# A ternary feed-forward sublayer whose last product runs in two float32r halves instead of one float32 product

## The chip, the cores and the metric

The kernel runs on one core of a Trainium2 chip. The metric is the device time of one execution, in microseconds (us). A core has five engines that matter here, each with its own in-order queue: PE (the matrix engine; its weight loads have a row of their own, PEld), DVE (VectorE), ACT (ScalarE), POOL (GpSimd) and SP, which only issues DMAs here. Engines wait for each other by semaphores. PE's results land in PSUM, from where DVE and ACT take them.

## The reference

The program is a decoder of four layers with three sublayers each (attention, cross attention, feed-forward) on x of 64 x 64 rows and width 256, that is 4096 rows. After each sublayer comes `x = layernorm(x + sublayer(x))`. The change is in the sixth sublayer, the feed-forward of the second layer:

```python
def _L1_ffn_ref(x, W_g, W_u, W_d):
    def rms_norm(x, eps=1e-8):
        mean = jnp.mean(x, axis=-1, keepdims=True)
        var = jnp.var(x, axis=-1, keepdims=True)
        return (x - mean) / jnp.sqrt(var + eps)
    def activation_quant(x):
        s = 127.0 / jnp.max(jnp.abs(x), axis=-1, keepdims=True)
        return jnp.clip(jnp.round(s * x), -128, 127) / s
    def ternary_matmul(x, w):
        return jnp.matmul(x, jnp.sign(w).T)
    xq = activation_quant(rms_norm(x))
    p = jax.nn.silu(ternary_matmul(xq, W_g)) * ternary_matmul(xq, W_u)
    return ternary_matmul(p, W_d)
```

All three weights are used by their signs only (-1, 0 or 1). The hidden width is 1024. The rows xq are whole numbers times one scale per row, so the first two products are exact in bf16; the gated rows p are full float32 numbers.

## The kernel before

The 4096 rows are eight groups of 512 (`NTOK`), four tiles of 128 each (`TG`). The hidden width is eight chunks of 128 (`HC`). `l1_ffn` walks over 64 units (group g, chunk i), one a step, and each step records work for several units at different stages:

- `hidden(g, i)` (L1378 to L1381): four bf16 products of 512 columns on PE give the PSUM banks "gate" and "up", DVE multiplies gate by the row scales into the SBUF tile `hid` (L1380), ACT applies Silu in place (L1381).
- `gated` one step later (L1386): DVE multiplies `hid` by "up", in place.
- `down` two steps behind `hidden` (L1396): for each of the four row tiles, PE takes 128 columns of `hid` as stationary weights and streams 256 columns of the signs of W_d, both float32, and adds into the PSUM tiles `acc` over the eight chunks. One float32 product of the program stands as two LDWEIGHTS and two MATMUL in the trace.
- `ends` of a finished group, spread over the steps of the next: `sums` (L1411, DVE: z = acc * scale + x), statistics (L1417, L1419), `root` (L311 on DVE and a power on POOL, L313), `apply` (L1428 on ACT).
- `first.quantize` of a later group, in three parts at the steps i = 6, 2 and 5: row statistics on DVE (L339, L342, L311) and then on POOL a power (L313) and four normalisations (L228); row maxima on DVE (L233 to L236) and four roundings on POOL (L240); clipping on DVE (L243, L244). `first.turn` (L266 to L275) then transposes a group's quantized rows.

The order on PE and DVE in this stage is the order in which the code records it (`manual_schedule`); ACT, POOL and SP are ordered by a planner, but each runs its own queue in order. The end of the cross attention's last group (`inverted`, `fetched`, `added`, `normalized`, L1280 to L1300: a reciprocal on DVE, two DMAs, then two products of 1024 columns and four normalisations on POOL) falls into the first steps of this stage.

The signs are made during the cross attention (`L1Ffn.weights`, L207 and L210): twelve pieces of 512 columns, POOL compares with 0 from below, one step later DVE compares from above and subtracts. The signs of W_g and W_u go to a bf16 tile, those of W_d are written over the float32 weight. All weight tiles come from `ring`, a pool of eight slots of 2048 float32 columns; the loads of the following sublayer's weights (`l2_wqkv`, `l2_wsg`) wait for slots of it. `l2_wqkv` is also scaled once on DVE (L1507) while the cross attention still runs.

The pool tiles `hid` have five buffers, the PSUM banks gate and up four together, `acc` two.

Of the kernel before, what the change touches and what calls it, by code (L numbers as in the profile page):

```python
# [9 lines left out]

F32 = mybir.dt.float32
BF16 = mybir.dt.bfloat16
FP8 = mybir.dt.float8e4
I32 = mybir.dt.int32
AF = mybir.ActivationFunctionType
ALU = mybir.AluOpType
# [3 lines left out]
P = 128  # L20
# [3 lines left out]
NTOK = TG * P  # L24
# [3 lines left out]
WCOLS = 2048  # L28
# [3 lines left out]
class Linear:  # L32
# [68 lines left out]
    def first(self, pool, bank, fill):  # L101
# [74 lines left out]
class L1Ffn:  # L176
# [9 lines left out]
    def load(self):  # L186

        dec, names = self.dec, ("l1_wg", "l1_wu", "l1_wd")
        self.raw = [dec.weight(name) for name in names]
        both = dec.ring.tile([P, 2, WCOLS], BF16, tag="w", name="l1_signs")  # L190
        self.out = [both[:, 0], both[:, 1], self.raw[2]]
        self.signs = []
        for w, out, name in zip(self.raw, self.out, names):
            n = dec.ins[name].shape[1]
            dec.load(w.rearrange("p (c n) -> p c n", n=n), dec.ins[name].rearrange("(c p) n -> p c n", p=P))
            self.signs.append(out.rearrange("p (c n) -> p c n", n=n))

    def weights(self):

        nc, N = self.nc, 512  # L200
        chunks = [(w[:, c : c + N], out[:, c : c + N]) for w, out in zip(self.raw, self.out) for c in range(0, WCOLS, N)]
# [77 lines left out]
class Decoder:  # L279
# [1082 lines left out]
    def l1_ffn(self, ctx, shared, later, first):  # L1362
# [7 lines left out]
        wg, wu, wd = first.signs  # L1370
        state = first.state

        def hidden(g, i):
            xt, rows, _ = state[g]
            pg, pu = self.bank("gate"), self.bank("up")
            for ps, w in ((pg, wg), (pu, wu)):
                for c in range(2):
                    nc.tensor.matmul(ps, w[:, c, i * P : (i + 1) * P], xt[:, c, :], start=c == 0, stop=c == 1)  # L1378
            h = wk.tile([P, NTOK], F32, tag="hid", name="hid", bufs=5)
            nc.vector.tensor_tensor(h, pg, rows, ALU.mult)  # L1380
            nc.scalar.activation(h, h, AF.Silu)  # L1381
            state[g, i] = h, pu

        def gated(g, i):
            h, pu = state[g, i]
            nc.vector.tensor_tensor(h, h, pu, ALU.mult)  # L1386

        def down(g, i):

            h = state.pop((g, i))[0]  # L1390
            if i == 0:
                state[g, "acc"] = [
                    self.psum.tile([P, 2, D], F32, tag="acc", name="acc", bufs=2) for _ in range(2)
                ]
            for t in range(TG):
                nc.tensor.matmul(  # L1396
                    state[g, "acc"][t // 2][:, t % 2, :], h[:, t * P : (t + 1) * P], wd[:, i, :],
                    start=i == 0 and t % 2 == 0, stop=i == HC - 1, skip_group_check=True,
                )

        def ends(g):

            x, am, acc = self.X[g], state.pop(g)[2], state.pop((g, "acc"))
            z = wk.tile([P, TG, D], F32, tag="z", name="z")
            mv = self.smallp.tile([P, TG, 2], F32, tag="bnmv", name="bnmv", bufs=4)
            st = self.smallp.tile([P, TG, 6], F32, tag="bnst", name="bnst", bufs=4)
            rstd, nb = self.small(TG, "rstd", bufs=4), self.small(TG, "nmr", bufs=4)

            def sums():
                for t in range(TG):  # L1410
                    nc.vector.scalar_tensor_tensor(  # L1411
                        z[:, t, :], acc[t // 2][:, t % 2, :], am[:, t : t + 1], x[:, t, :], ALU.mult, ALU.add
                    )

            def statistics(ts):
                for t in ts:
                    nc.vector.bn_stats(st[:, t, :], z[:, t, :])  # L1417
                for t in ts:
                    nc.vector.bn_aggr(mv[:, t, :], st[:, t, :])  # L1419

            def root():
                statistics((2, 3))
                self.rsqrt(rstd, mv[:, :, 1], 1.0, 1e-5)

            def apply():
# [1117 lines left out]
```

## Time and profile before

| | |
|---|---|
| device time, median of 3 runs | 4253.46 us (4248.44 to 4256.29) |
| span of the profiled execution, first to last instruction | 4250.0 us |
| mean granted PE clock of that execution | 0.986 |
| feed-forward stage: first and last L1380 on DVE | 1135.0 and 1314.3 us |
| PE busy in the span | 4051.5 us, 95% |
| DVE, ACT, POOL busy in the span | 3042.7, 2106.4, 1506.3 us |

Times of instructions count from the span's start. A busy share is an average over stages with different limits, so the stage is read by itself in windows of one group's length. "Idle before" is the time in which an engine waited before an instruction, with what ended that wait. MATMUL records overlap: a record lasts longer than the distance to the next start, and it is the distance that the engine needs for one.

### The profile page before, as it was taken

How to read it: one execution, taken by the hardware profiler on the slowest of the kernel's cores; microseconds unless marked ns; L12 is line 12 of the kernel's file. 1: busy time of each engine (PE TensorE's matmuls, PEld its weight loads, DVE VectorE, ACT ScalarE, POOL GpSimd, SP SyncE). 2: the span in 40 equal slices, each digit the busy share in tenths (PEclk: the TensorE clock that was granted, in tenths of full speed). 3: DMA queues.
4: the chain of work that ended last, by engine and by line, in shares of the span. 5: the costliest groups of instructions: out<-in, count | busy, mean ns of one | idle time of the engine just before them, and what ended most of it. 6: DMA issues, size and time to landing. Idle time of an engine off the chain costs nothing.

```text
span 4250.0 us, 74130 instructions
## 1 busy us (share of the span) xinstructions
PE 4051.5 (95%) x28788; PEld 2618.4 (62%) x28808; DVE 3042.7 (72%) x6107; ACT 2106.4 (50%) x3863; POOL 1506.3 (35%) x1553
## 2 busy tenths in 40 slices
PE   8889999989998999989999999999999999999998
PEld 5645556666675555546666666666656666666666
DVE  6844548888685688877777777777766777777786
ACT  5555635767634577544444444444433444444443
POOL 4511112242341111115555555555544444444111
PEclk9989999999999999999999999999999999999999
DMA  2200002333300000031111111111131100000000
GB/s 81 73 21 10 1 26 69 72 84 71 82 1 12 1 1 1 10 132 28 26 31 26 26 31 26 26 30 27 26 102 28 26 23 21 23 23 16 11 16 18
DMA packets 108294, 144.00 MB, mean 34 GB/s; under 512 B 15844, under 2 KB 73380, under 8 KB 106536
## 3 DMA queue, kind: packets, MB, share of 16 engines
q1 hardware_dynamic: 106984, 137.69, 12.7%
q8 instruction: 228, 3.74, 0.4%
q10 hardware_dynamic: 960, 1.57, 0.2%
q14 instruction: 122, 1.00, 0.1%
HBM read 70.25 MB, written 26.76 MB: 23 GB/s over the span
## 4 chain that ended last, share of the span: by engine, by line
PE 65%; DVE 15%; ACT 6%; POOL 4%; issue 3%; DMA 1%; SPq 0%; POOLq 0%; ACTq 0%; DVEq 0%
PE p L1777 19%; PE acc L2066 5%; PE acc L2274 4%; PE sq L1208 3%; PE ret L1247 2%; PE qT L319 2%; PE acc L1396 2%; POOL rstd L313 2%; DVE bnst L339 2%; PE gate L911 2%; DVE mc L1213 2%; PE gate L1592 2%; PE sk L1211 2%; PE s L2004 2%; PE up L911 2%
## 5 line engine op out<-in xcount | busy, mean ns | idle before, releaser
L313 POOL TENSOR_TENSOR rstd<-rstd,neg_half 128x1 f32<-128x1 f32 (+1 forms) x195 | 157.9, 810 | 653.1 <-DVE rstd L311 585.2
L313 POOL TENSOR_TENSOR hrq<-hrq,neg_half 128x4 f32<-128x4 f32 x256 | 258.7, 1011 | 300.7 <-DVE hrq L311 283.9
L1213 DVE TENSOR_REDUCE mc<-sq 128x2 f32<-128x512 f32 x512 | 317.1, 682 | 63.9 <-PE sk L1211 63.7
L1219 ACT ACTIVATE e<-sk 128x512 f32<-128x512 f32 x512 | 265.5, 608 | 112.1 <-PE sk L1211 111.5
L1208 PE MATMUL sq<-l1x 32*128 32x256 f32 x2048 | 275.2, 407 | 4.9 <-DVE z L1094 3.1
L1777 PE MATMUL p<-l3a_wq,xt 128*128 128x512 f32 x512 | 243.8, 599 | 11.2 <-DVE v L300 9.9
L313 POOL TENSOR_TENSOR hrk<-hrk,neg_half 128x4 f32<-128x4 f32 x160 | 188.2, 1176 | 185.8 <-DVE hrk L311 181.0
L1211 PE MATMUL sk<-l1x 32*128 32x256 f32 x2048 | 252.9, 392 | 0.0
L1777 PE MATMUL p<-l3a_wk,xt 128*128 128x512 f32 x512 | 247.1, 605 | 0.0
L1208 PEld LDWEIGHTS sq<-l1x 32*128 32x128 f32 x2048 | 208.3, 195 | 58.8 <-issue 23.6
L1777 PE MATMUL p<-l3x_wq,xt 128*128 128x512 f32 x512 | 242.3, 596 | 0.3 <-DVE k L2168 0.3
L1777 PE MATMUL p<-l3a_wv,xt 128*128 128x512 f32 x512 | 233.9, 599 | 0.4 <-ACT y L94 0.4
L2274 PE MATMUL acc<-l3x_wo,yt 128*128 128x256 f32 x1024 | 232.4, 380 | 1.6 <-DVE yt L300 1.0
L2066 PE MATMUL acc<-l3a_wproj,yt 128*128 128x256 f32 x1024 | 232.0, 379 | 0.5 <-DVE yt L300 0.5
L2066 PEld LDWEIGHTS acc<-l3a_wproj,yt 128*128 128x128 f32 x1024 | 194.2, 190 | 53.7 <-issue 29.2
L2274 PEld LDWEIGHTS acc<-l3x_wo,yt 128*128 128x128 f32 x1024 | 190.5, 190 | 33.9 <-issue 7.7
L1211 PEld LDWEIGHTS sk<-l1x 32*128 32x128 f32 x2048 | 188.5, 187 | 7.3 <-issue 2.9
L2237 POOL TENSOR_TENSOR s<-s,smx 128x512 f32<-128x512 f32 x64 | 66.9, 1046 | 333.8 <-DVE smx L2236 319.8
L319 PEld LDWEIGHTS qT<-ident,q 128*128 128x128 f32 x1024 | 121.9, 141 | 95.9 <-issue 75.2
L2050 POOL TENSOR_TENSOR hry<-hry,neg_half 128x8 f32<-128x8 f32 x64 | 106.2, 1659 | 183.4 <-DVE hry L2046 183.4
L319 PE MATMUL qT<-ident,q 128*128 128x128 f32 x1024 | 157.4, 277 | 3.3 <-ACT qT L2208 2.4
L1247 PE MATMUL ret<-e,vt 128*32 128x256 f32 x2048 | 140.6, 390 | 18.2 <-DVE mc L1213 17.2
(415 smaller groups left out, 10209.4 us busy)
## 6 DMA issues: line engine op xcount, KB each, us to landing
vs<-v SPq DMA_DIRECT2D x308, 128.0 KB
l3x_kv<-kv SPq DMA_DIRECT2D x28, 256.0 KB
x<-in_x SPq DMA_DIRECT2D x8, 512.0 KB
ct<-in_ctxT SPq DMA_DIRECT2D x8, 512.0 KB
cn<-in_ctx SPq DMA_DIRECT2D x8, 512.0 KB
l1x<-in_ctx SPq DMA_DIRECT2D x128, 32.0 KB
l1x_x<-x SPq DMA_DIRECT2D x8, 512.0 KB
l1x<-l1x_x SPq DMA_DIRECT2D x128, 32.0 KB
```

Source lines behind the costliest of these rows:

```text
L313: nc.gpsimd.tensor_tensor(out, out, self.neg_half[:, :n], ALU.pow)
L319: self.nc.tensor.transpose(ps[:, j * P : (j + 1) * P], blk, self.ident)
L911: nc.tensor.matmul(ps[:n], w[:, c, h0 : h0 + n], xt[:, c, :], start=c == 0, stop=c == 1)
L1208: nc.tensor.matmul(ps[:, n, :], x_[rows, j, part], c_[rows, j, :], start=True, stop=True)
L1211: nc.tensor.matmul(ps[:, n, :], c_[rows, j, part], x_[rows, j, :], start=True, stop=True)
L1213: nc.vector.tensor_reduce(mc[new % 2][:, ra + k, 2 * j : 2 * j + 2], ps, AX.X, ALU.max, negate=True)
L1219: nc.scalar.activation(es[rb + k], ps, AF.Exp, scale=scale)
L1247: nc.tensor.matmul(ret[32 * r : 32 * r + 32, :], vt[i % 2][:, lc, 4 * r + j, :], es[r][:, lc, :], start=lc == 0, stop=lc == 1,)
L1777: self.nc.tensor.matmul(ps, lhs(c), w(c, cols), start=c == 0, stop=c == 1 and bias is None)
L2050: nc.gpsimd.tensor_tensor(r, r, self.neg_half[:, :8], ALU.pow)
L2066: nc.tensor.matmul(acc[:, :D], yts[h % 2][:, h // 2, :], wp[n // 8][:, (n % 8) * D : (n % 8 + 1) * D], start=n == 0, stop=n == 15,)
L2274: nc.tensor.matmul(acc[:, :D], yts[h % 2][:, h // 2, :], w.o[n // 8][:, (n % 8) * D : (n % 8 + 1) * D], start=n == 0, stop=n == 15,)
```

## The change

The signs of W_d go to a new tile of type float32r from the ring, asked for when the ninth piece is made. [...] `down` makes two float32r products, one for each half, where there was one float32 product, and stands three steps behind `hidden` instead of two. `sums` moves from step 1 to step 2 of the next group. `hid` has four buffers, `hhi` two, `hlo` three.

```diff
 class L1Ffn:  # load
-        self.out = [both[:, 0], both[:, 1], self.raw[2]]
+        self.out = [both[:, 0], both[:, 1], None]
...
         def step(i):
             if i < len(chunks):
+                k, cols = chunks[i]
                 below[i] = self.shared.tile([P, N], F32, tag="below", name="below", bufs=2)
-                nc.gpsimd.tensor_scalar(below[i], chunks[i][0], 0.0, None, ALU.is_lt)
+                nc.gpsimd.tensor_scalar(below[i], self.raw[k][:, cols], 0.0, None, ALU.is_lt)
             if i > 0:
-                w, out = chunks[i - 1]
-                nc.vector.scalar_tensor_tensor(out, w, 0.0, below[i - 1], ALU.is_gt, ALU.subtract)
+                k, cols = chunks[i - 1]
+                if self.out[k] is None:
+                    self.out[k] = self.dec.weight("l1_wd_signs", F32R)
+                nc.vector.scalar_tensor_tensor(
+                    self.out[k][:, cols], self.raw[k][:, cols], 0.0, below[i - 1], ALU.is_gt, ALU.subtract
+                )
...
-            h = wk.tile([P, NTOK], F32, tag="hid", name="hid", bufs=5)
+            h = wk.tile([P, NTOK], F32, tag="hid", name="hid", bufs=4)
...
         def gated(g, i):
-            h, pu = state[g, i]
+            h, pu = state.pop((g, i))
             nc.vector.tensor_tensor(h, h, pu, ALU.mult)
+            hi, lo = (wk.tile([P, NTOK], F32R, tag=n, name=n, bufs=b) for n, b in (("hhi", 2), ("hlo", 3)))
+            nc.scalar.copy(hi, h)
+            nc.gpsimd.tensor_tensor(lo, h, hi.bitcast(F32), ALU.subtract)
+            state[g, i] = hi, lo
...
             for t in range(TG):
-                nc.tensor.matmul(
-                    state[g, "acc"][t // 2][:, t % 2, :], h[:, t * P : (t + 1) * P], wd[:, i, :],
-                    start=i == 0 and t % 2 == 0, stop=i == HC - 1, skip_group_check=True,
-                )
+                for k in range(2):
+                    nc.tensor.matmul(
+                        state[g, "acc"][t // 2][:, t % 2, :], h[k][:, t * P : (t + 1) * P], wd[:, i, :],
+                        start=i == 0 and t % 2 == 0 and k == 0, stop=i == HC - 1 and k == 1, skip_group_check=True,
+                    )
...
-            return {1: sums, 3: lambda: statistics((0, 1)), 4: root, 6: apply}
+            return {2: sums, 3: lambda: statistics((0, 1)), 4: root, 6: apply}
...
-                if 2 <= n <= N + 1:
-                    down(*units[n - 2])
-                    if units[n - 2][1] == HC - 1:
-                        end = ends(units[n - 2][0])
+                if 3 <= n <= N + 2:
+                    down(*units[n - 3])
+                    if units[n - 3][1] == HC - 1:
+                        end = ends(units[n - 3][0])
```

More of the change, by code (lines that the diff above doesn't have):

```diff
@@ L11 @@
 F32 = mybir.dt.float32
+F32R = mybir.dt.float32r
 BF16 = mybir.dt.bfloat16
@@ L190, in load, with signs @@
         both = dec.ring.tile([P, 2, WCOLS], BF16, tag="w", name="l1_signs")
-        self.out = [both[:, 0], both[:, 1], self.raw[2]]
-        self.signs = []
-        for w, out, name in zip(self.raw, self.out, names):
+        self.out = [both[:, 0], both[:, 1], None]
+        for w, name in zip(self.raw, names):
             n = dec.ins[name].shape[1]
             dec.load(w.rearrange("p (c n) -> p c n", n=n), dec.ins[name].rearrange("(c p) n -> p c n", p=P))
-            self.signs.append(out.rearrange("p (c n) -> p c n", n=n))
+    def signs(self):
+        dec, names = self.dec, ("l1_wg", "l1_wu", "l1_wd")
+        return [o.rearrange("p (c n) -> p c n", n=dec.ins[name].shape[1]) for o, name in zip(self.out, names)]
     def weights(self):
         nc, N = self.nc, 512
-        chunks = [(w[:, c : c + N], out[:, c : c + N]) for w, out in zip(self.raw, self.out) for c in range(0, WCOLS, N)]
+        chunks = [(k, slice(c, c + N)) for k in range(3) for c in range(0, WCOLS, N)]
         below = [None] * len(chunks)
@@ L1369, in l1_ffn @@
         wk = ctx.enter_context(self.tc.tile_pool(name="l1f", bufs=2, reuse_waits="tile"))
-        wg, wu, wd = first.signs
+        wg, wu, wd = first.signs()
         state = first.state
@@ L1384, in gated @@
         def gated(g, i):
-            h, pu = state[g, i]
+            h, pu = state.pop((g, i))
             nc.vector.tensor_tensor(h, h, pu, ALU.mult)
+            hi, lo = (wk.tile([P, NTOK], F32R, tag=n, name=n, bufs=b) for n, b in (("hhi", 2), ("hlo", 3)))
+            nc.scalar.copy(hi, h)
+            nc.gpsimd.tensor_tensor(lo, h, hi.bitcast(F32), ALU.subtract)
+            state[g, i] = hi, lo
         def down(g, i):
-            h = state.pop((g, i))[0]
+            h = state.pop((g, i))
             if i == 0:
```

## Prediction

> **What bounds the kernel now.** I first read the page's busy shares (PE 95% of the span), then, since the diff touches one sublayer, the busy times of each engine in windows of one group's length in that stage. Columns: window, length, busy time (instructions) of PE, PEld, DVE, ACT, POOL, then granted clock and DMA.
>
> ```profile
> 1156.00:1178.00 22.00, 18.74 (x77) 13.42 (x79) 16.85 (x44) 5.04 (x9) 19.18 (x17) 0.92 0.00 1
> 1178.00:1200.00 22.00, 21.89 (x111) 16.49 (x112) 18.58 (x46) 8.29 (x14) 9.04 (x11) 1.00 0.00 0
> 1200.00:1222.00 22.00, 21.89 (x111) 16.47 (x113) 18.58 (x46) 8.39 (x14) 8.70 (x10) 1.00 0.01 1
> ```
>
> From 1178 on PE has no gap (21.89 of 22.00): PE sets the pace, 22.1 us a group. But DVE is behind it by little, 18.58 us. That is the most a faster PE could uncover: 3.5 us a group. Second, the groups by form in the stage (busy us, mean ns, idle before), and an addition of two full tiles on POOL elsewhere (min/median/max ns):
>
> ```profile
> L1396 PE MATMUL acc<-l_wd,hid 128*128 128x256 f32 x512 | 122.6, 383 | 0.4
> L228 POOL TENSOR_SCALAR work<-x,bnmv,rstd 128x256 f32<-128x256 f32 x28 | 33.8, 1223 | 0.6
> L313 POOL TENSOR_TENSOR rstd<-rstd,neg_half 128x4 f32<-128x4 f32 x15 | 15.6, 1043 | 63.2 <-DVE rstd L311 63.2
> L2161 POOL TENSOR_TENSOR k<-k,biases x14: 1267/1270/1276, 3223.8 to 3848.9; 128x512 f32<-128x512 f32 x14
> ```
>
> The 256 float32 products of the program are 512 passes. Third, the timeline of one group, POOL and then PE (start, length, [idle before]):
>
> ```profile
> 1204.88 1.01 POOL L313 TENSOR_TENSOR rstd<-rstd,neg_half 128x4 f32<-128x4 f32 x1 [5.45 <-DVE rstd L311]
> 1206.00 4.83 POOL L228 TENSOR_SCALAR work<-x,bnmv,rstd 128x256 f32<-128x256 f32 x4
> 1216.22 1.84 POOL L240 TENSOR_SCALAR work<-work,qs 128x256 f32<-128x256 f32 x4 [5.39 <-DVE am L236]
> ...
> 1202.73 1.89 PE L1396 MATMUL acc<-l_wd,hid 128*128 128x256 f32 x8
> 1204.46 0.38 PE L1378 MATMUL gate<-xt,l_signs 128*128 128x512 bf16 x1
> ```
>
> POOL's work comes in bursts that nobody waits for today: the power and four normalisations hold it from 1204.88 to 1210.83, 5.95 us, while PE goes on. Eight passes of `down` go from 1202.73 to 1204.46: 0.216 each. Last, one place where PE did stand (timeline of PE, then two windows):
>
> ```profile
> 1171.65 0.59 PE L1378 MATMUL up<-xt,l_signs 128*128 128x512 bf16 x2 [3.15 <-DVE hid L1380]
> 1172.25 3.59 PE L1396 MATMUL acc<-l_wd,hid 128*128 128x256 f32 x8
> ...
> 1168.50:1171.65 3.15, 0.00 (x0) 0.00 (x0) 2.98 (x13) 0.02 (x1) 2.39 (x5) 1.00 0.00 0
> 1172.48:1175.89 3.41, 3.41 (x9) 2.40 (x9) 2.81 (x11) 0.63 (x1) 3.41 (x4) 0.50 0.02 5
> ```
>
> After 3.15 us of standing the granted clock is 0.50 for 3.41 us, and the same eight passes take 3.59 us instead of 1.89.
>
> **The change, part by part.** *PE.* A unit's eight float32 passes become eight float32r passes (two halves, four row tiles). The trace has no float32r. Lower end: the rate of the bf16 products of gate and up, whose 512 columns start 0.216 apart, so 0.108 for 256 columns; float32 weight loads don't stop that much, since the eight float32 passes of L271 fit into 0.95 us (1201.78 to 1202.73). Upper end: float32, 0.216, no gain. I take 0.109: a half of 12 bits should need one pass where the whole number needs what costs four bf16 passes. So `down` goes from 1.73 to 0.87 us a unit, 6.9 us a group, and PE's own need to 15.2 us a group.
>
> The Trainium skill, "FP8 and Floating Point Precision", TensorE Precision Notes, says that true float32 goes four times through the array while reduced-precision float32 is read as four bytes and cut to about 22 bits. That speaks for the lower end; no run here shows it.
>
> *ACT.* `hhi` adds one copy of 128x512 a unit, 0.59 us (L275's row, 588 ns): 4.7 a group on an engine busy 8.3 of 22. Covered by ACT's idle time; only its place in a chain counts, 0.6.
>
> *POOL.* `hlo` adds one subtraction of two full SBUF tiles a unit: L2161's row, 1.27 us (lower end 1.04, L2237's product of the same shape with a broadcast factor). Eight make 10.2 us a group, POOL's need is 8.7 + 10.2 = 18.9. On average it fits. But the queue is in order, and the rebuilt order of POOL's instructions puts, in each group, the power and the four normalisations of step 6 in front of `hlo` of chunk 6. Now follow one group. At time 0 DVE has the variances (L311):
> - POOL: 0.08 to its start, 5.95 for power and normalisations, 1.27 for `hlo` of chunk 6: 7.3 us.
> - Meanwhile PE gets through about two steps of 1.74 us, up to `hidden` three units on, and then stands at `down` of chunk 6, which waits for that `hlo`. Everything behind it on PE waits too: the next gate and up, hence DVE's L1380, Silu, and all later halves. The `hid` buffer of chunk 6, needed four units later, hangs on the same `hlo`. DVE runs dry after three more units.
> - Released, PE does `down`, 0.87, and the next gate; from gate's start to DVE's start is 0.63 now (1187.52 to 1188.15): 1.5 us.
> - DVE then has, until the next L311 is done: ten multiplications at 0.60, `sums` 1.65, L233 to L236 1.62, statistics and root 0.88 + 0.99 + 0.17, clipping 1.39, statistics for the next group 2.49 (all distances between starts in that timeline): 15.2 us. In that time POOL has seven `hlo`, four roundings and a power, 11.8 us, and PE five steps and a turn, 10 us; both fit.
>
> The circle is 7.3 + 1.5 + 15.2 = 24.0 us, against 22.1: plus 1.9. PE stands about 4 us in it, more than the 3.15 that halved the clock above. Price of that: 0 to 1.7 (3.59 - 1.89); I take 1.3, since `down` and gate after the stop, 1.3 us, run at half speed on the circle. So 25.3 a group, plus 3.2; for the five groups from 1185.6 to 1296.2, plus 16.
>
> The Trainium skill, "SBUF — State Buffer", SBUF: two separate sides, adds a rule against the change: POOL shares a port pair with DVE's two-port operations, and the later one is held off for the whole instruction. In this trace L228's 32 records spread from 1215 to 1232 ns with DVE's products beside them, so the rows show none of it. DVE's clipping, 1.39 us a group, would be the candidate; by the rule the sum could grow by up to 1.39 x 7 = 9.7 us.
>
> *First two groups.* They take 50.6 us today (1135.0 to 1185.6), with POOL full (19.18 of 22.00) behind the DMA of the last cross attention rows. Sixteen `hlo` join the same queue: 0 to +10, I take +5, since eight of them (10.2) meet 2.8 us of free POOL time in the second window, but the first window has 14 us free.
> *Last group and drain.* With nothing left to quantize DVE needs 16.5 us in 22 (window from 1288): 0 to -5.5, I take -3. The extra chunk of delay, copy and subtraction at the drain: 0 to +3, I take +2.
> *Ring.* The new tile takes the slot that `l2_wqkv`'s load took. In SP's queue that load moves behind the next tile's loads and stores, to where `l2_wsg` stands (871.7), and `l2_wsg` moves further back, where nothing needs it for 200 us. DVE's scaling of `l2_wqkv` (L1507) started 5.0 us after the load's issue (856.8, 861.8), so now at 876.7; in DVE's queue it stands after the second piece of W_d, free at 874.4. DVE, 27.8 busy of 30 there, waits 2.2 us, with the row maxima L1213 and the PSUM banks of PE behind it: 0 to +2.5, I take +2.
> *At nothing:* `sums` one step later (`acc` is asked for again one step after it, as now; in the circle DVE reaches it 1.2 us after its release, and if it were late the first `down` of the next group would stand by as much) and the signs in float32r (same instruction, same size).
>
> Sum: 16 + 5 - 3 + 2 + 2 = +22. The profiled span was 4250.0, 3.5 below the median 4253.5, to which I add: 4275.5.
>
> **Rivals.** *DVE becomes the bound, POOL hides* (faster). Speaks for it: POOL's average, 18.9, fits. Then a group is 18.6 plus some 0.5: -3 in six groups, first groups 0, drain and ring +4: 4239. It needs the burst plus `hlo` within the slack that two steps leave, at most 4.5 us; they are 7.3. Against: the queue order.
> *It cancels.* No clock price, `hlo` at 1.04 and the burst shorter by a micro or two through ACT or POOL overlap: the circle comes to 22, the rest to 0: 4254.
> *float32r runs at float32's pace* (the change doesn't do what it says). The circle's hop grows by 0.87 to 24.9, PE needs 22.1 besides its standing of 4: about 26, at half clock 1.7 more: +5.6 x 5 = 28, plus 5 and 4, no gain at the end: +37, 4291.
> *Main case*, its own bounds: without clock price and with `hlo` 1.04, 1.7 x 5 - 3 + 4 = +9; with 1.7 of clock price and +10 in the first groups, +30.
>
> **Numbers.** Main 0.74, 4275.5. Faster rival 0.08, cancelling 0.08, float32's pace 0.10. Range 4261 to 4293: it leaves out the faster rival, most of the cancelling and little above. Under 0.2% (8.5 us) can't be told from no change here. Slower by more: 0.74 x 0.97 + 0.10 = 0.82; within: 0.10; faster: 0.08.
>
> **What would show it.** Right: L1396's successor starts 0.109 apart; POOL 18 to 19 of a group's 25; PE waiting 4 us or more for POOL `hlo` once a group, and the clock at 0.50 after it; DVE dry just before. Wrong: PE and DVE windows both near 18.6 of 19 would be the faster rival; starts 0.216 apart the float32 pace. If POOL's subtraction takes far from 1.27, the circle's term for it is wrong.

## The result: 1.4% slower

The changed kernel takes 4311.09 us (median of 4 runs, 4308.62 to 4314.06) beside 4252.16 for the kernel before on the same chip (4 runs, 4248.44 to 4256.29): ratio 1.0139, interval 1.0125 to 1.0154, some 59 us. Its profiled execution has a span of 4306.8 us, 56.8 more, at a mean granted clock of 0.981. L1380 of before (gate times rows on DVE) is L1389 now; by its starts the span divides like this:

| stretch | before | after | difference | in the forecast |
|---|---|---|---|---|
| up to the first gate product | 1135.0 | 1134.1 | -0.9 | +2 |
| first two groups | 50.6 | 62.4 | +11.8 | +5 |
| five groups after them | 110.6 | 138.5 | +27.9 | +16 |
| last group, to its last gate product | 18.1 | 28.3 | +10.2 | -3 |
| from there to the end | 2935.7 | 2943.5 | +7.8 | +2 |
| span | 4250.0 | 4306.8 | +56.8 | +22 |

In these lines `hhi` is the gated rows copied by ACT into a float32r tile, and `hlo` what POOL gets by subtracting that copy from them, `hid - hhi`. The windows of one old group's length, now of the changed kernel (window, length, busy time and instructions of PE, PEld, DVE, ACT, POOL, granted clock, DMA share, GB/s):

```profile
1156.00:1178.00 22.00, 12.34 (x65) 9.12 (x65) 10.17 (x26) 6.32 (x10) 16.09 (x13) 0.77 0.00 2
1178.00:1200.00 22.00, 14.36 (x77) 10.12 (x78) 15.93 (x42) 10.96 (x19) 17.64 (x17) 0.77 0.01 1
1200.00:1222.00 22.00, 15.46 (x76) 11.48 (x78) 15.17 (x37) 7.30 (x12) 14.21 (x14) 0.78 0.00 1
1222.00:1244.00 22.00, 16.34 (x91) 11.94 (x92) 13.33 (x32) 10.11 (x18) 15.53 (x16) 0.91 0.00 0
```

No engine is full any more: PE is down from 21.89 to between 12.3 and 16.3, DVE from 18.58 to between 10.2 and 15.9, POOL has 14 to 18, and the clock is below 1 in every window. So the time is in waiting for one another. Who waits is in the groups by form of the stage (busy us, mean ns, idle before and what ended it):

```profile
L1398 POOL TENSOR_TENSOR hlo<-hid,hhi 128x512 fp32r<-128x512 f32 x62 | 81.1, 1315 | 58.6 <-ACT hhi L1397 51.1 <-issue 6.8
L1410 PE MATMUL acc<-l_wd_signs,hhi 128*128 128x256 f32 x243 | 80.8, 357 | 0.0
L1410 PE MATMUL acc<-l_wd_signs,hlo 128*128 128x256 f32 x243 | 70.2, 315 | 51.4 <-POOL hlo L1398 51.2
...
L1389 DVE TENSOR_TENSOR hid<-gate,rows 128x512 f32<-128x512 f32 x64 | 43.8, 684 | 74.6 <-PE gate L1387 60.9 <-PE ret L1256 11.7 <-PE acc L1410 2.0
...
L1397 ACT CAST hhi<-hid 128x512 fp32r<-128x512 f32 x62 | 38.3, 618 | 63.9 <-PE acc L1410 57.5 <-POOL hlo L1398 4.9 <-PE gate L1387 0.3
```

A ring of waits: PE's `down` for POOL's `hlo` (51.2), DVE for PE's gate (60.9), POOL for ACT's `hhi` (51.1), and ACT's `hhi` for PE's `down` (57.5). The last wait is for a buffer: `hhi` has two, and one is free again when the `down` that reads it is through. The products with `hhi` wait for nothing. One group shows the ring's order. POOL, then PE, then DVE, from timelines of the changed kernel (start, length, what, [idle before]):

```profile
1252.28 1.01 POOL L322 TENSOR_TENSOR rstd<-rstd,neg_half 128x4 f32<-128x4 f32 x1
1253.40 4.84 POOL L237 TENSOR_SCALAR work<-x,bnmv,rstd 128x256 f32<-128x256 f32 x4
1258.21 2.51 POOL L1398 TENSOR_TENSOR hlo<-hid,hhi 128x512 fp32r<-128x512 f32 x2
...
1279.08 1.30 POOL L1398 TENSOR_TENSOR hlo<-hid,hhi 128x512 fp32r<-128x512 f32 x1 [3.41 <-ACT hhi L1397]
1280.34 1.01 POOL L322 TENSOR_TENSOR rstd<-rstd,neg_half 128x4 f32<-128x4 f32 x1
...
1259.53 0.39 PE L1410 MATMUL acc<-l_wd_signs,hlo 128*128 128x256 f32 x1 [4.15 <-POOL hlo L1398]
...
1261.76 0.69 DVE L1389 TENSOR_TENSOR hid<-gate,rows 128x512 f32<-128x512 f32 x1 [5.54 <-PE gate L1387]
...
1270.83 1.19 DVE L320 TENSOR_SCALAR rstd<-bnmv 128x4 f32<-128x4 f32 x1
...
1277.97 0.17 DVE L320 TENSOR_SCALAR rstd<-bnmv 128x4 f32<-128x4 f32 x1
```

From power to power: 7.25 us on POOL until PE is let go (1252.28 to 1259.53), 2.23 until DVE has a gate, 16.38 until the second L320 is done (1278.14), and 2.20 more to the power, which now stands behind one `hlo` that waited for ACT. That is 28.06 here. The forecast's circle is there, with its four stations. Two things in it are new: L320 (DVE's addition of 1e-5 ahead of a power, 128 x 4 elements, once for the residual and a second time for the quantizer) takes 1.19 us at 1270.83 and 0.17 at 1277.97, and the last station was 0.08 in the forecast. Over these groups either the second L320 is long too, or the power is late.

The clock, in windows of the changed kernel with the columns of above, while PE stands and after it is let go, in this group and in the last:

```profile
1255.40:1259.50 4.10, 0.00 (x0) 0.00 (x0) 0.82 (x2) 0.63 (x1) 4.10 (x5) 1.00 0.00 0
1260.50:1264.00 3.50, 3.50 (x15) 2.47 (x14) 1.89 (x4) 1.25 (x2) 1.49 (x2) 0.54 0.00 0
1337.30:1348.90 11.60, 0.01 (x1) 0.01 (x1) 1.60 (x5) 0.65 (x2) 1.70 (x3) 0.71 0.00 0
1348.90:1352.40 3.50, 3.50 (x12) 2.49 (x13) 0.66 (x2) 0.62 (x1) 2.26 (x2) 0.50 0.00 0
```

After each of these two stands PE goes on for 3.5 us at about half clock (0.54 and 0.50). The 11.6 us of the third line have another cause. POOL and PE in the last group, from timelines of the changed kernel:

```profile
1333.35 1.30 POOL L1398 TENSOR_TENSOR hlo<-hid,hhi 128x512 fp32r<-128x512 f32 x1 [2.20 <-ACT hhi L1397]
1340.39 0.38 POOL L55 PARTITION_ALL_REDUCE allmaxw<-wmax  x1 [5.74 <-issue]
1347.58 2.49 POOL L1398 TENSOR_TENSOR hlo<-hid,hhi 128x512 fp32r<-128x512 f32 x2 [6.82 <-issue]
...
1348.89 0.58 PE L1410 MATMUL acc<-l_wd_signs,hlo 128*128 128x256 f32 x1 [11.63 <-POOL hlo L1398]
```

The all-reduce belongs to the seventh sublayer (`Linear`, the maximum of its weight); the planner lets it run as soon as its input is there. It is short, but POOL is lost for 5.74 us before and 6.82 us after it, with "issue" as the reason and two MODIFY_POOL_CONFIG records at the head of each stretch (1334.60 and 1340.72). What POOL does in the two stretches the records don't show. Before the change the same instruction ran at 1293.40 with nobody behind it. Now a subtraction is.

### The profile page after: what moved, and what is told of

Read it like the earlier page. It is cut to its first block, busy times and chain, and to the rows that moved or that the text cites. A ratio compares the mean times of both kernels' runs of the same rounds, so it can differ in the third digit from the quotient of the medians.

```text
span 4306.8 us, 74356 instructions
## 1 busy us (share of the span) xinstructions
PE 4028.2 (94%) x28788; PEld 2599.0 (60%) x28808; DVE 3053.2 (71%) x6107; ACT 2143.2 (50%) x3927; POOL 1592.4 (37%) x1617
## 3 DMA queue, kind: packets, MB, share of 16 engines
q14 instruction: 124, 1.02, 0.1%
## 4 chain that ended last, share of the span: by engine, by line
PE 61%; DVE 16%; ACT 6%; POOL 6%; issue 3%; DMA 1%; SPq 0%; POOLq 0%; DVEq 0%; ACTq 0%
PE p L1791 19%; PE acc L2080 5%; PE acc L2288 4%; PE sq L1217 2%; PE qT L328 2%; POOL rstd L322 2%; DVE bnst L348 2%; PE ret L1256 2%; PE gate L920 2%; DVE mc L1222 2%; PE gate L1606 2%; PE s L2018 2%; PE up L920 2%; PE up L1606 2%; PE acc L1622 1%
## 5 line engine op out<-in xcount | busy, mean ns | idle before, releaser
L1217 PEld LDWEIGHTS sq<-l1x 32*128 32x128 f32 x2048 | 208.4, 194 | 57.2 <-issue 21.6
```

The costliest lines, as they stand in the source:

```text
L1217: nc.tensor.matmul(ps[:, n, :], x_[rows, j, part], c_[rows, j, :], start=True, stop=True)
```

## The experiments

Each kernel is the changed one with one edit, unless it says otherwise. "Groups" are distances between gate products as in the table above: first two together, mean of the five after them, last. The ratio is to the kernel before on the same chip. Each edit shifts the line numbers, so one instruction has another L in each run.

| edit | time us | ratio, interval | first two | a middle group | last |
|---|---|---|---|---|---|
| kernel before | 4252.16 | | 50.6 | 22.1 | 18.1 |
| changed kernel | 4311.09 | 1.0139, 1.0125-1.0154 | 62.4 | 27.7 | 28.3 |
| e1 no subtraction | 4240.86 | 0.9970, 0.9957-0.9983 | 47.3 | 19.85 | 13.4 |
| e7 high half only | 4235.28 | 0.9957, 0.9942-0.9972 | 46.2 | 18.8 | 12.8 |
| e4 normalisations on ACT | 4290.97 | 1.0087, 1.0071-1.0104 | 57.4 | 24.6 | 28.4 |
| e15 burst split on POOL | 4290.43 | 1.0083, 1.0070-1.0097 | 59.5 | 24.9 | 28.4 |
| e5 subtraction on DVE | 4286.20 | 1.0079, 1.0064-1.0094 | 55.4 | 26.1 | 19.5 |
| e2 addition as TENSOR_TENSOR | 4310.68 | 1.0142, 1.0125-1.0159 | 62.9 | 27.75 | 28.3 |
| e11 addition on ACT | 4303.15 | 1.0110, 1.0096-1.0124 | 62.2 | 26.05 | 27.4 |
| e3 all-reduce later | 4301.07 | 1.0111, 1.0096-1.0126 | 62.5 | 27.7 | 15.8 |
| e8 before, products later | 4264.50 | 1.0023, 1.0013-1.0032 | 51.1 | 23.1 | 18.1 |
| e14 the same, scales apart | 4257.73 | 1.0011, 1.0001-1.0020 | 52.3 | 22.1 | 18.1 |
| e16 changed, scales apart | 4304.98 | 1.0120, 1.0105-1.0136 | 61.8 | 26.6 | 29.5 |
| e9 POOL in program order | 4305.99 | 1.0118, 1.0104-1.0132 | 60.6 | 27.2 | 28.5 |
| e17 all, normalisations on POOL | 4285.51 | 1.0073, 1.0061-1.0086 | 58.5 | 26.0 | 14.7 |
| e10 three edits | 4272.95 | 1.0051, 1.0036-1.0066 | 56.3 | 23.6 | 15.7 |
| e12 all, spread | 4261.33 | 1.0015, 1.0007-1.0024 | 55.2 | 22.8 | 14.6 |
| e18 e12, statistics at step 6 | 4257.58 | 1.0010, 1.0001-1.0019 | 54.3 | 21.7 | 14.6 |

**Is it POOL at all?** The theory: PE and DVE wait for POOL's queue. The rivals: the many short passes on PE, or the extra chunk of delay.

```diff
 e1
-            hi, lo = (wk.tile([P, NTOK], F32R, tag=n, name=n, bufs=b) for n, b in (("hhi", 2), ("hlo", 3)))
+            hi = wk.tile([P, NTOK], F32R, tag="hhi", name="hhi", bufs=5)
             nc.scalar.copy(hi, h)
-            nc.gpsimd.tensor_tensor(lo, h, hi.bitcast(F32), ALU.subtract)
-            state[g, i] = hi, lo
+            state[g, i] = hi, hi
 e7: the same, but
+            state[g, i] = (hi,)
...
-                for k in range(2):
+                for k in range(1):
```

> Left out: the subtraction, so the low half is never computed; the second pass of each pair reads the high half again. PE issues the same passes and weight loads, ACT the same copies, and the output weight's products run one chunk later as in the changed kernel. Theory (POOL's queue is what PE and DVE wait for): with no subtraction on POOL nothing stands behind the power and the four normalisations, the five middle groups fall from 27.7 us to 18-21, the first two from 62.4 to 45-51, the last from 28.3 to 17-20, and the time from 4311 to 4235-4260. Rival (the sixteen short passes a chunk, with a weight load each, set the pace on PE): same passes, so 26-28 us a group and 4300-4311. Rival (the extra chunk of delay): also unchanged, 4300-4311.

> Left out: the low half as a whole, its subtraction and its four passes a chunk; copy of the high half and the delay stay. Beside the kernel that only leaves out the subtraction it takes 32 passes a group off PE, about 3.8 us at 0.119. Theory (PE is not the bound once POOL is out of the way, DVE is): 0-1.5 us a group less than that kernel, so within 12 us of its time. Rival (passes and weight loads on PE are dear): 3.8 us a group or more less, 27 us or more in all.

With the same passes, weight loads, copies and delay, a middle group falls by 7.85 us to 19.85, below the kernel before. So both rivals fall. But e1 and e7 take away two waits at once: they also give `hhi` five buffers, and ACT's copy, which waits 24.4 us for `down` in the five middle groups of the changed kernel, no longer waits for it at all. How the 7.85 us divide between the subtraction and the buffers these two runs don't show; e18 below, with the subtraction on POOL and two buffers, bounds it. The window of a group in e1, columns as above:

```profile
1200.00:1222.00 22.00, 19.02 (x125) 13.98 (x125) 20.38 (x51) 14.78 (x27) 9.97 (x12) 1.00 0.00 1
```

The clock is whole and DVE is the fullest engine, 20.38 of 22. Taking 32 passes a group off PE as well (e7, 3.8 us of PE at 0.119) saves only 1.0 a group. In e1 one pass of `down` starts 0.119 after the other (median), in the changed kernel 0.120, in the kernel before 0.216: float32r runs near the forecast's lower end, 0.108.

**POOL's order or POOL's work?** e4 takes the four normalisations off POOL; e15 leaves POOL every instruction and changes their order only.

```diff
 e4, in quantize, ahead of the four normalisations on POOL
+            if not whole:
+                if t0 == 0:
+                    st["nb"] = dec.small(TG, "nmr", bufs=4)
+                    nc.vector.scalar_tensor_tensor(
+                        st["nb"], st["mv"][:, :, 0], -1.0, st["rstd"], ALU.mult, ALU.mult
+                    )
+                for t in (t0, t0 + 1):
+                    nc.scalar.activation(
+                        work[:, t, :], x[:, t, :], AF.Identity,
+                        bias=st["nb"][:, t : t + 1], scale=st["rstd"][:, t : t + 1],
+                    )
+                return
 e15, in l1_ffn (names of engines shortened)
-        with self.tc.manual_schedule(engines={PE, DVE}):
+        with self.tc.manual_schedule(engines={PE, DVE, Pool}):
...
-                if i == 6:
-                    stage(g + 2, 0)      # statistics, power, four normalisations
+                at = {0: (0, 1), 1: (2,), 3: (3,), 6: (4,)} if g == 0 else {0: (2,), 2: (3,), 5: (4,)}
+                for k in at.get(i, ()):
+                    stage(g + 1, k)
+                if i >= 6:
+                    stage(g + 2, i - 6)  # 6: statistics, power; 7: two; 0 of the next group: two
```

> The four normalisations of the next but one group's rows go from POOL to ACT (scale and bias a row, one small DVE operation more). Theory (the circle of 7.2 us POOL, 2.7 us hop and half clock, 16.8 us DVE, 1.0 us before the power): 4.8 us of POOL's 7.2 leave the circle and PE no longer stands long enough to lose its clock, so 21-24 us a group for 27.7; five groups -18 to -33, first two -5 to -8, last unchanged near 28; time 4265-4288. Rival (the f32r passes or the delay set the pace): 26-28 us a group, 4300-4311. Rival (ACT's copies of the high half are the tight chain): ACT has 1.7 us a group more, so 28-30 us a group, 4311-4325.

> POOL keeps every instruction of the changed kernel; only their order is other: in program order, with the four normalisations as two pairs, a step apart, so that a subtraction stands ahead of each pair. Theory (the burst of power and four normalisations ahead of a subtraction, 7.2 us, is what the circle pays): the first subtraction after the power ends 4.8 us sooner, PE stands less than 2 us and keeps its clock, 22.5-25.0 us a group for 27.7, last group unchanged near 28, time 4268-4292. Rival (it is the sum of POOL's work and its handshakes with ACT, not the order): 26.5-28 us a group, 4300-4311.

e15 gets 2.8 us a group from the order alone, with POOL's work unchanged: the burst ahead of a subtraction is real. The 24.9 lie within the 22.5 to 25.0 expected, near their upper end, and 0.5 of the 2.8 is POOL's program order, which e9 below has without the split. Its POOL and PE in one group, and its window (timelines and windows of e15):

```profile
1246.90 1.28 POOL L1400 TENSOR_TENSOR hlo<-hid,hhi 128x512 fp32r<-128x512 f32 x1 [0.90 <-ACT hhi L1399]
1248.16 2.43 POOL L237 TENSOR_SCALAR work<-x,bnmv,rstd 128x256 f32<-128x256 f32 x2
1250.56 1.27 POOL L1400 TENSOR_TENSOR hlo<-hid,hhi 128x512 fp32r<-128x512 f32 x1
1251.81 2.42 POOL L237 TENSOR_SCALAR work<-x,bnmv,rstd 128x256 f32<-128x256 f32 x2
...
1251.88 0.39 PE L1412 MATMUL acc<-l_wd_signs,hlo 128*128 128x256 f32 x1 [1.56 <-POOL hlo L1400]
1255.52 0.39 PE L1412 MATMUL acc<-l_wd_signs,hlo 128*128 128x256 f32 x1 [1.54 <-POOL hlo L1400]
...
1246.00:1270.40 24.40, 17.73 (x112) 12.37 (x113) 21.34 (x46) 13.14 (x23) 19.17 (x18) 1.00 0.00 0
```

PE now stands twice for 1.5 us in place of once for 4.15, and its clock stays whole. e4 has little more, 3.1 a group, though it takes the four normalisations off POOL, and it misses its 4265 to 4288 by a little. Its trace names the wait that came instead, on the small DVE operation that e4 adds (timelines of e4, DVE and then POOL):

```profile
1270.18 0.16 DVE L239 SCALAR_TENSOR_TENSOR nmr<-bnmv,rstd 128x4 f32<-128x4 f32 x1 [3.20 <-POOL rstd L334]
...
1267.90 1.28 POOL L1410 TENSOR_TENSOR hlo<-hid,hhi 128x512 fp32r<-128x512 f32 x1 [3.39 <-ACT hhi L1409]
1269.14 1.00 POOL L334 TENSOR_TENSOR rstd<-rstd,neg_half 128x4 f32<-128x4 f32 x1
```

DVE stands for the power, the power behind a subtraction, the subtraction for ACT. e5 takes the subtraction itself to DVE:

```diff
 e5
+        def rest(g, i):  # one step after gated
+            hi, lo, h = state[g, i]
+            nc.vector.tensor_tensor(lo, h, hi.bitcast(F32), ALU.subtract)
...
+                if 2 <= n <= N + 1:
+                    rest(*units[n - 2])
```

> The subtraction goes from POOL to DVE, one chunk after the product, so that DVE need not wait for ACT's copy. Theory (POOL's queue out, DVE full): DVE had some 19 us of work in the 19.85 us group of the kernel without a subtraction; eight more of 0.60 us start to start make 23.7-25.0 us a group, the first two groups 50-56, the last 16-20, no 1.19 us TENSOR_SCALAR any more; time 4255-4280. Rivals (PE pace, delay): 26-28 us a group, 4295-4311.

It has 26.1 a group, above its 23.7 to 25.0, and 4286 us, above its 4255 to 4280: the subtraction is dear there too. DVE is nearly full without it (e1), and in e5 it also waits 13.1 us in the five middle groups for ACT's copy.

**What makes L320 seven times as long?** Beside a subtraction on POOL it takes 1.19 to 1.21 us in eight of eight cases, and each time ends 0.02 to 0.03 after the subtraction; without one it takes 0.17 in eight of eight. e2 does the residual's addition by another DVE instruction, e11 on ACT.

```diff
-                self.rsqrt(rstd, mv[:, :, 1], 1.0, 1e-5)  # on DVE the addition, on POOL the power
+                nc.vector.tensor_tensor(rstd, mv[:, :, 1], eps, ALU.add)                        # e2
+                nc.scalar.activation(rstd, mv[:, :, 1], AF.Identity, bias=eps[:, 0:1])          # e11
+                nc.gpsimd.tensor_tensor(rstd, rstd, self.neg_half[:, :TG], ALU.pow)             # e2, e11
```

> The addition of 1e-5 ahead of the residual's reciprocal root is made by DVE as a TENSOR_TENSOR with a tile of constants, in place of the TENSOR_SCALAR that took 1.19 us for 0.17 whenever a subtraction ran on POOL. Theory (that TENSOR_SCALAR stands until POOL's instruction ends, and DVE's stretch of the circle is 1.6 us longer than forecast mostly by it): the new instruction takes 0.15-0.25, the five middle groups fall from 27.7 to 26.5-27.0, the time from 4311 to 4301-4307. Rival (it is late for a reason of its own, such as its input): the new instruction takes 1 us too and nothing changes, 4308-4314. Rival (PE pace): 0.17, but nothing gained.

> The addition of 1e-5 ahead of the residual's reciprocal root goes from DVE to ACT, so that no small DVE instruction with all its operands in SBUF stands at that place; a TENSOR_TENSOR in its stead had been held for 1.18 us just as the TENSOR_SCALAR was. Theory (DVE instructions that read SBUF alone, by two operands or as a TENSOR_SCALAR, stand until POOL's subtraction ends): DVE's next product starts 1.0 us sooner and the five middle groups fall from 27.7 to 26.4-27.0, time 4300-4308. Rival (the hold passes to the next such instruction, or POOL's stretch takes the time back): 27.4-27.8 us a group, 4307-4314.

My theory fell in e2: I had held the form TENSOR_SCALAR responsible, and the TENSOR_TENSOR is held just as long. DVE in e2 and ACT in e11 (timelines):

```profile
1272.17 1.18 DVE L1439 TENSOR_TENSOR rstd<-bnmv,eps 128x4 f32<-128x4 f32 x1
```

```profile
1273.25 0.30 ACT L1439 ACTIVATE rstd<-bnmv,eps 128x4 f32<-128x4 f32 x1 [0.18 <-DVE bnmv L1435]
```

On ACT it is not held, and a middle group falls by 1.65 us: 1.02 is the hold; besides, the power is 0.08 behind the second L320 in the groups from 1228 on, where it was 2.2 to 2.5 late in every other one. The second L320 stays on DVE in e11 and is held there still, 1.05 to 1.06 in four groups.

What is held in these rows is DVE's TENSOR_SCALAR and two-input instructions with all their operands in SBUF: L320, and in one case each L244 and L1440, 0.98 for 0.17 and 0.16. Reading SBUF alone is not enough: the maxima (L242, TENSOR_REDUCE) take 1.21 beside a subtraction in seven of seven cases, as they did before the change without one, and L1431 (BATCH_NORM_STATS2) 0.42 in six of six, for 0.39 to 0.42 without. The gate and up products read PSUM, and run their 0.67 to 0.69 beside a subtraction in 63 of 63. The Trainium skill, "SBUF — State Buffer", SBUF: two separate sides, has a rule for this: DVE operations in a two-port mode, or with two inputs in SBUF against a POOL operation that reads SBUF, and POOL's operations take one port pair for a whole instruction, the other side standing by until it ends. e2's TENSOR_TENSOR has two inputs in SBUF, and its 1.18 against 0.16 agrees with the rule; whether L320's TENSOR_SCALAR runs in a two-port mode no run here shows. The other way round it is POOL that waits: a subtraction that starts during DVE's clipping takes 1.66 for 1.28.

**The last group.** e3 takes the weight's maximum out of POOL's queue here, and with it DVE's scaling of that weight (0.49 us).

```diff
-        self.ws, rws = self.all_max(col, "w")      # Linear.__init__
+        m, r = self.all_max(self.both, "x")        # Linear.scales: both maxima in two columns
```

> The maximum over partitions of the seventh sublayer's weight is taken together with that of its input, so that its library load and its all-reduce leave POOL's queue in this stage. Theory (the load holds the subtractions of the last group): last group 28.3 us to 18-22, the other groups unchanged, time 4311 to 4296-4306. Rivals (PE pace, delay): last group unchanged at 27-28, time within 3 us of 4311.

The last group falls from 28.3 to 15.8 us, further than expected, and the others don't move. So the all-reduce with the stretches before and after it costs 12.5 us there; without it the last group is 2.3 shorter than before the change.

**The delay.** e8 is the kernel before with nothing of the change but the later products and sums, and with six buffers for `hid`; e14 moves the quantizer's scales a step up in it; e16 puts e14's second edit on the changed kernel.

```diff
 e8, on the kernel before
-            h = wk.tile([P, NTOK], F32, tag="hid", name="hid", bufs=5)
+            h = wk.tile([P, NTOK], F32, tag="hid", name="hid", bufs=6)
...
-                if 2 <= n <= N + 1:
-                    down(*units[n - 2])
+                if 3 <= n <= N + 2:
+                    down(*units[n - 3])
-            return {1: sums, 3: lambda: statistics((0, 1)), 4: root, 6: apply}
+            return {2: sums, 3: lambda: statistics((0, 1)), 4: root, 6: apply}
 e14, on e8, and e16, on the changed kernel
-                if i == 2 and g >= 1:
+                if i == 1 and g >= 1:
                     stage(g + 1, 1)  # row maxima, scales, roundings
```

> The kernel before, with the output weight's products one chunk later and the sums one step later, as in the change, and nothing else of it (six buffers for the hidden rows in place of five). Theory (the delay only lengthens the drain): 22.1 us a group as before, +1 to +3 us in all, 4253-4258. Rival (the delay costs the groups): 24-28 us a group, 4270-4311.

> The kernel before with the products one chunk later (which by itself had 23.1 us a group for 22.1), and the quantizer's scales at step 1 in place of step 2, so that DVE's four sums and its scales no longer stand in the same step. Theory (the change pushed the sums, 1.7 us of DVE, into the step that has the scales, 1.6 us): back to 22.0-22.4 us a group, 4251-4258. Rival (the delay itself, through buffers or PSUM): 23.0-23.2 us a group, 4258-4266.

> The changed kernel with the quantizer's scales at step 1 in place of step 2, apart from the four sums. In the kernel before with later products this edit gave back 0.96 us a group. Theory (in the changed kernel POOL, not DVE's step, sets that place: the normalisations end at 1258.2 and the scales follow at 1265.0, so they can go a step up with the circle as long as before): 27.2-27.9 us a group, 4306-4313. Rival (the doubled step is on the circle here too): 26.5-26.9 us a group, 4301-4306.

The delay was not free: 0.96 us a group in e8, where I had expected none. e14 gives all of it back, so it is not the delay but the step in which `sums` now falls: DVE's 1.7 us of sums and 1.6 of maxima and scales stand one after the other while PE waits for the next product. e16 gives 1.1 on the changed kernel, the rival's figure, not mine: with the scales a step up DVE does them while it waits for the gate.

**The second group.** e9 keeps POOL to the program's order, which moves two subtractions ahead of the two z operations of the cross attention's last group.

```diff
-        with self.tc.manual_schedule(engines={PE, DVE}):
+        with self.tc.manual_schedule(engines={PE, DVE, Pool}):
```

> POOL's queue in the stage in the order in which the program issues it. It differs from the changed kernel at one place alone: in the second group two subtractions stand ahead of the two z operations (some 2.34 us each), not behind them. Theory (POOL's order is what the second group pays): the first two groups fall from 62.5 to 56-60, the rest stays at 27.7 and 28.3, time 4304-4309. Rival (the second group is slow for the clock or its first transposes): 62-63 us, 4308-4314.

The second group falls from 37.9 to 34.9, the first two together by 1.9, less than expected. The middle groups come down by 0.5 too, which I hadn't expected: three of the five are alike now, 27.2, with both L320 held (DVE's stretch 17.0 to 17.3 us, that is 15.2 and two holds of 1.02) and the power never late.

**All together.** e10 joins e3, e2 and e4 with the normalisations a step behind their power; e17 joins e3, e11, e15 and e16; e12 joins e3, e11 and e4 in two pairs a step apart, with the quantizer's statistics at step 7, its scales at step 3 and the residual's statistics in one step; e18 is e12 with the statistics back at step 6.

```diff
 e12
...
+                at = {0: 0, 1: 1, 2: 2, 3: 3, 6: 4} if g == 0 else {0: 1, 1: 2, 3: 3, 5: 4}
+                if i in at:
+                    stage(g + 1, at[i])
+                if i == 7:           # e18: 6
+                    stage(g + 2, 0)
```

> Three edits together on the changed kernel: the maximum of the seventh sublayer's weight taken with that of its input, the addition of 1e-5 as a TENSOR_TENSOR, and the four normalisations on ACT; these and the small DVE operation before them moreover stand one step after their power, since with them on ACT alone DVE's small operation waited 3.2 us for the power, which stood behind a subtraction on POOL. Theory (the circle through POOL's queue is all that lengthens the groups): 20.5-22.5 us a group, first two groups 48-55, last 13-16, time 4240-4262. Rivals (PE pace, delay): 24-28 us a group in spite of it, 4280 or more.

> All on the changed kernel, with the normalisations left on POOL: program order and split pairs there, scales at step 1, the addition of 1e-5 on ACT, one all-reduce for both maxima. Theory (burst, hold, doubled step and library load are what the change pays): 20.5-23.0 us a group, first two groups 50-57, last 13-16, time 4240-4266. Rival (ACT's and POOL's handshakes for each half keep a group near 23.5 us whatever the order): 23.2-25 us, 4268-4280.

> The changed kernel with all that was found: one all-reduce for both maxima; the addition of 1e-5 on ACT; the normalisations on ACT, in two pairs a step apart, a step behind their power; the scales one step behind the sums, and the statistics of the residual in one step. Theory (POOL's queue, DVE's hold and the doubled step are all that lengthens the groups; what is left is some 19 us of DVE work): 19.8-21.8 us a group, first two groups 46-54, last 13-16, time 4228-4252, so level with the kernel before or below it. Rival (with the passes on PE and the copies on ACT there is another tight chain near 23.5 us): 22.8-24 us a group, 4262-4275.

> The kernel of e12 with one thing other: the next group's row statistics (2.5 us of DVE) stand at step 6 again, where PE turns the next group and DVE waited 3.39 us a group for the gate in e12. Theory (DVE's own work is the bound that is left, and e12 only moved it out of a hole that PE makes anyway): 20.3-21.6 us a group for 23.5, time 4244-4256, level with the kernel before. Rival (PE's turn and the half clock after it are the bound, DVE's wait there costs nothing): 23.0-23.7 us a group, 4258-4265.

All four missed what was expected of them, e18 by little: e10 has 23.6 a group for 20.5 to 22.5, e12 22.8 for 19.8 to 21.8, and e17, with 26.0 for 20.5 to 23.0, does worse than e15 alone. I had made a new wait there, DVE's maxima at step 1 for POOL's second pair, which program order puts behind a subtraction (DVE in e17, a timeline):

```profile
1228.11 1.22 DVE L241 TENSOR_REDUCE am<-work 128x4 f32<-128x1024 f32 x1 [5.34 <-POOL work L236]
```

So the causes don't add up like terms; each edit moves work into a place where something else may stand. e12 and e18 differ in one number, the step of the row statistics, and show the same from the good side: in e12 DVE stands 3.2 to 3.4 us for the gate in three of the five groups while PE turns the next group, in e18 the statistics fill that hole, and a group falls from 22.8 to 21.7. e18 just misses both its expected figures, 21.6 a group and 4256, with 21.7 and 4257.58; its time is 0.1% above the kernel before (1.0010, 1.0001 to 1.0019). It is the best version with both halves; e1 and e7 are faster than the kernel before, but they leave out the low half. e18 also bounds what the two buffers of `hhi` cost: with the subtraction on POOL and the two buffers kept, ACT's copy waits 1.8 us for `down` in the five groups instead of 24.4, and a group is 0.4 shorter than before the change. So most of that wait came with PE's standing. How much of the 1.9 a group between e18 and e1 is the buffers' stays open: no run has a third one with the subtraction on POOL.

## Why the forecast was right and wrong

*Right.* The direction, and the circle as its cause: POOL's power and four normalisations ahead of a subtraction, PE standing for it, the clock at half after that, DVE dry. POOL's station was put at 7.3 us and is 7.25; the hop from PE's release to DVE's gate, with half clock, at 2.8 and 2.2 to 2.9; `hlo` at 1.27 and 1.277 (median); a float32r pass at 0.109 and 0.120. The 0.109 rested on halves of 12 bits, a width that no run shows; what the runs show is the pass. The first step of a unit is longer, 0.306, so `down` takes 1.14 us a unit (e1, median) and not 0.87, and PE is busy 16.9 us a group in e1 where 15.2 was forecast: a term too small, but PE isn't the bound. ACT's copy takes 0.618 for 0.59. The three rivals didn't come: float32r is not at float32's pace, POOL doesn't hide, and nothing cancels. (The main case's upper bound was put at +30; its own terms give 3.6 x 5 + 10 - 3 + 4 = +29.)

Of the 34.8 us between the forecast's +22 and the span's +56.8, the last group has 13.2, the five middle groups 11.9, the first two 6.8 and the end 5.8; the ring took 2.9 less.

*Wrong: the circle's DVE stretch and its last station, 25.3 forecast, 27.7 measured, 12 us in five groups.* DVE's 15.2 us were distances between starts in the trace of before, where no subtraction runs beside them. With one, L320 stands 1.02 longer once or twice a group, or else the power stands 2.2 to 2.5 behind an `hlo`; the stretch is 16.4 to 17.4. The rule on the shared port pair was in front of me, but I tried it on L228's rows, which are POOL's one-input normalisations beside products from PSUM, pairs that show no hold, and took the clipping for the candidate. The trace of before had the answer beside L2161, the very line that priced `hlo` (timelines of before, POOL and then DVE):

```profile
3250.40 1.26 POOL L2161 TENSOR_TENSOR v<-v,biases 128x512 f32<-128x512 f32 x1
...
3250.46 1.24 DVE L311 TENSOR_SCALAR hrk<-hrk 128x4 f32<-128x4 f32 x1
```

L311 (now L320) takes 1.24 us there in all fourteen cases in which it meets L2161, and 0.15 to 0.17 on this tile with nothing on POOL. `sums` a step later was costed at nothing; by e8 it is 0.96 a group on the kernel before, and by e16 the doubled step is on the changed kernel's circle as well.

*Wrong: the last group, -3 forecast, +10.2 measured.* The working looked at DVE's need alone. The trace of before shows the all-reduce at 1293.40 on POOL, in time for nobody; that POOL's queue had something else in it at this place, and what it costs to those behind it, was left out. With it away (e3) the term is -2.3, near the forecast's -3.

*Too small: the first two groups, +5 forecast, +11.8 measured.* The second group alone pays 10.5 (37.9 for 27.4). PE stands 8.86 us there, behind the burst and the two z operations, and the clock is 0.77 in both windows. I had offered POOL's free time to the subtractions without asking where in the queue it lies. e9 shows 3.0 of the second group to be the z operations' place, and in e1, without the subtraction and with five buffers for `hhi`, the second group has 24.3.

*The end and the ring.* The ring's +2 didn't show (-0.9): DVE waited 1.03 us for the load of `l2_wqkv` and not 2.2, and over all profiles this stretch ends between 1130 and 1144, so a term of 2 us can't be read from one of them. Of the +7.8 behind the last gate product about 1.8 is the drain, as forecast: the first row sums of the next stage start 50.8 us later than before, the last gate product 49.0 later. The rest comes in stages that compute the same as before. The largest piece is at the hand-over near 3240; windows of before, then of the changed kernel:

```profile
3185.00:3200.00 15.00, 12.23 (x66) 7.40 (x65) 8.08 (x17) 3.98 (x8) 9.66 (x9) 0.96 0.00 0
```

```profile
3236.80:3256.00 19.20, 15.56 (x62) 9.25 (x62) 8.19 (x18) 3.94 (x8) 9.67 (x9) 0.74 0.00 0
```

DVE and POOL have the same work in both, 4.2 us apart in length, and the granted clock is 0.96 and 0.74: the half clock came to lie on the path. All the other profiles have 2939 to 2948 us in this part, so some us of it vary from run to run whatever the edit. No run tests why, and it stays open.

## What to carry to other kernels

Work given to an idle engine is priced by its place in that engine's queue, not by the engine's mean: look for every burst, and every rare instruction, that will stand ahead of it, and at what the planner is free to put there. A trace gives an instruction's length beside its old neighbours; a two-input POOL instruction was a new neighbour for DVE's TENSOR_SCALAR and two-input instructions in SBUF, and the same pair stood elsewhere in the trace of before. And where an engine will wait, ask how long in one piece: the same normalisations in two pairs cost 2.3 us a group less than in one at the same program order (e15 beside e9), and PE stood 1.5 us twice and kept its clock.

## What the runs showed of the hardware

- A float32r pass of 256 columns starts 0.119 to 0.120 us after the one before, with a weight load for each (216 ns mean, overlapped), against two such steps of 0.216 for a float32 product.
- A DVE instruction of 128x4 elements takes 1.18 to 1.21 us in place of 0.17 while POOL subtracts two SBUF tiles, as TENSOR_SCALAR and as TENSOR_TENSOR; a product of 128x512 with a PSUM operand isn't held by it (63 of 63), nor is a TENSOR_REDUCE of 128x1024 from SBUF (1.21 us, seven of seven).
- One PARTITION_ALL_REDUCE between subtractions costs POOL's queue 5.74 us before it and 6.82 after it, each behind two MODIFY_POOL_CONFIG records.
- PE's clock stays at 1.00 when it stands twice for 1.5 us in a group of 24.4 us, and is 0.54 over the 3.5 us from 1260.5, after PE stood 4.15.
